# A four-layer block on one core: attention's output projection one unit later, skip terms and gate one slot later

## Chip, core and metric

One Trainium2 chip, one of its cores. The metric is the device time of one execution in microseconds (us), the median of the timed runs. A profile is one more execution, taken by the hardware profiler.

## What is computed

The program is a chain of four layers on an image batch x of shape 2 x 128 x 64 x 64 (channels first, 4096 pixels per image), all in float32. The change touches the first layer, a selective state-space network, and the second, attention. The third is attention with 1x1 projections, the fourth mixes four scales. Cut to what matters:

```
# layer 0, twice (two inner layers), t2 = layernorm(t)
u, z = split(t2 @ in_w.T);  u = silu(causal_conv4(u))
dt, Bm, Cm = split(u @ xproj_w.T);  dt = softplus(dt @ dt_w.T + dt_b)
h[t] = exp(dt[t]*A) * h[t-1] + dt[t]*u[t]*Bm[t]        # 256 channels x 16 states
y = sum_over_states(h * Cm) + u * ssm_D                # + skip term
t = t + (y * silu(z)) @ out_w.T                        # gate, mixer's output
t = t + gelu(layernorm(t) @ w1.T + b1) @ w2.T + b2
# layer 1
q, k, v = conv3x3(x)
attn = softmax(q.T @ k / sqrt(128));  out = attn @ v.T
x = x + Wo @ out + bo                                  # output projection
```

## The kernel before

**First layer (lines 111 to 533).** The pixels are cut into chunks of 512. An item is one image, one inner layer and one chunk: 32 items. The state runs on in the variable `carry` from chunk to chunk. An item has 32 slots, `t_` from 0 to 31. Every slot issues one scan (`scan`, VectorE, L384: 128 partitions are 32 channels times 4 states, 512 steps), and one exponential on ScalarE for the scan four slots ahead (`decay`, L373). Four slots make a group, 8 groups an item. At a group's end VectorE multiplies the next group's inputs (`times_b`, L366), into a tile `h` of which there are 5 buffers, and GpSimd saves the last column (L386) and multiplies the scanned states by C (L387). TensorE sums states two groups at a time (`y_pair`, L399, 8 matmuls, which are 16 instructions in the trace), which frees both groups' `h`, and spreads dt*u for a group into the one PSUM buffer `pdu` (`spread_dtu`, L360), which `times_b` of the group before has to have read.

All the rest of an item is *background*, given out by hand: `background(i)` fills a list for each of the 32 slots, and the loop at L514 issues, in every slot, first the scan's own work and then that list. All engines take their instructions in this order. In the lists, `n = i+1` is the item whose convolution is being prepared, `p = i-1` the one whose scan has just ended and `q = i-2` the one in the feed-forward part. The pieces that matter here:

- `y_out(i, j)` (L407, VectorE): skip term, `u = u*D + py`, for half j of the 256 channels. It needs all four groups of that half to have been summed by `y_pair`. Half 0 stands in the item's own slot 23, half 1 in slot 6 of the following item.
- `gate(p)` (L410, GpSimd): `z = z*u`, right behind half 1's `y_out`.
- `mix_out(p)` (L416 and L417, TensorE, slot 8): the mixer's output projection of the gated z, plus the residual by an identity matmul.
- `mix_add(p)` (L420, ScalarE, slot 10): copies it back into the image `xt`. Slot 11 holds `silu`, with two loads of activation tables.

**Attention (lines 547 to 863).** Four runs, two layers times two images, of 128 units; a unit is a quarter of the scores of 128 queries. Eight units make a group of 256 queries. Unit by unit the loop at L811 issues `score` (L709 on TensorE; VectorE copies PSUM out and takes maxima, L714), then the pieces of earlier groups: `product` (attention times v, L759), which lags 14 units, `exponentials`, `turn` (a transpose L739, then copies by GpSimd and DMAs from two queues), `divide` (L784, VectorE) in the unit with w = 5, where w is the unit's place in its group, and, in the first of the two layers only, `finish_mm` (L791, TensorE: Wo times the divided result `on`) and `finish` (L795, VectorE: bias and residual). In a unit, `finish_mm` comes behind the unit's scores and ahead of its `product`. Scores go through a pool of two PSUM buffers. Every 32 units, in the first layer, the inputs of the next 3x3 convolution are formed on VectorE in six consecutive units (L589 to L600).

**Last layer (lines 866 to 1233)** is not touched.

The order is the source's: `manual_schedule` keeps the instructions of every engine as written, and semaphores are put in where one engine needs another's result or a buffer.

Of the kernel before, what the change touches and what calls it, by code (L numbers as in the profile page):

```python
# [67 lines left out]
def tile_conv_seq(ctx: ExitStack, tc, x, consts, vecs, wemb, wlay, wconv, wdt, wqkv, wsmall, wms, out):  # L68
# [33 lines left out]
    def v1(name, i=0):  # L102
        return vec[:, VEC[name] + i : VEC[name] + i + 1]
# [7 lines left out]
    with ExitStack() as s, tc.manual_schedule():  # L111
# [25 lines left out]
        for l in range(NL):  # L137
            w = wp.tile([P, NWL - DI], F32, name=f"wl{l}")
# [7 lines left out]
            u = wp.tile([P, KC, DI], F32, name=f"wu{l}")  # L146
# [6 lines left out]
            for g in range(4):  # L153
                pa = mm.tile([P, NJ, DS], F32, name="pa", tag="mm")
                nc.tensor.matmul(pa.rearrange("p j n -> p (j n)"), lhsT=four(g), rhs=an, start=True, stop=True)
                for q in range(4):
                    at = slice(32 * q, 32 * q + 32)
# [38 lines left out]
        def has(i):  # L196
            return 0 <= i < NI
# [265 lines left out]
        def background(i):  # L463

            todo = [[] for _ in range(NSL)]

            def at(t, f, *a):
                todo[t].append((f, a))

            n, p, q, r = i + 1, i - 1, i - 2, i + 2  # L470
            if has(q):
                at(3, gelu, q)
                at(6, ffn_down, q, (0, 1)), at(7, ffn_down, q, (2, 3)), at(9, ffn_add, q)
                at(11, out_mm, q), at(12, out_add, q)
            if has(p):
                at(6, y_out, p, 1), at(6, gate, p)
                at(8, mix_out, p), at(10, mix_add, p)
            if has(n):
                at(0, pu_taps, n, 0, (0, 1)), at(1, pu_taps, n, 0, (2, 3)), at(2, pu_out, n, 0)
                at(3, pu_taps, n, 1, (0, 1)), at(4, pu_taps, n, 1, (2, 3)), at(5, pu_out, n, 1)  # L480
                at(13, xproj, n), at(14, xproj_out, n), at(14, spread_bc, n)
                at(15, dtproj, n, 0), at(16, dtproj, n, 1), at(17, soft_plus, n), at(18, dt_end, n)
            if has(i):
                at(1, pz_mm, i, 0), at(3, pz_out, i, 0)
                at(5, pz_mm, i, 1), at(6, pz_out, i, 1)
            if has(i) or has(n):
                at(11, silu, i, n)
            if i == -1:
                for k in range(3):
                    at(8 * k + 2, fold, k)  # L490
            pair = [(k, second) for k, second in ((p, True), (r, False)) if has(k)]
            if has(r):
                at(10, embed, r), at(11, embed_out, r)
            w, m = {}, len(pair)
            for k, (it, second) in enumerate(pair):
                at(12 + 2 * k, ln_centre, w, k, it)
                at(13 + 2 * k, ln_square, w, k, it)
                at(27, ln_spread, w, k, m), at(28, ln_scale, w, k, it)
                at(29, ln_shift, w, k, it, second)
            if pair:  # L500
                at(17, ln_var, w, m), at(18, ln_eps, w, m), at(19, ln_rs, w, m), at(20, ln_newton, w, m), at(21, ln_step, w, m)
            if has(p):
                for f in range(4):
                    at(30 + f // 2, ffn_up, p, f)
            if has(i):
                at(23, y_out, i, 0)
            return todo

        eps = wp.tile([P, 1], F32, name="eps")
# [36 lines left out]
    LAG = 14  # L546
    with ExitStack() as s, tc.manual_schedule():
# [22 lines left out]
        def load(which, half):  # L570
            slot = st["ring"] = (st.get("ring", -1) + 1) % 3
            where[which, half] = slot
            nc.sync.dma_start(uw[:, slot], ufold[which][:, 9 * half : 9 * half + 9, :])
# [82 lines left out]
        def keys(r):  # L656
            k = st["k"] = sp.tile([P, N], F32, name="k", tag="k")
            chunks(r, 1, lambda cc: k[:, cc * 4 * QG : (cc + 1) * 4 * QG])
# [27 lines left out]
        def queries(r, cc):  # L686

            for i in range(4):
                st["q", r, 4 * cc + i] = sp.tile([P, QG], F32, name="q", tag="q", bufs=5)
            outputs(*products(0), [st["q", r, 4 * cc + i] for i in range(4)], bias(r, 0))  # L690

        def query(r, grp):
            ps = psq.tile([P, QG], F32, name="pqq", tag="q")
            dense(r, 0, grp * QG, QG, ps)
            q = st["q", r, grp] = sp.tile([P, QG], F32, name="q", tag="q", bufs=5)
            put(q, ps, bias(r, 0))
# [19 lines left out]
        def exponentials(r, blk):  # L716
            scale = 1.0 if runs[r][0] else float(C) ** -0.5
            nm = sp.tile([P, 1], F32, name="nm", tag="nm", bufs=2)
            nc.vector.tensor_reduce(nm, st["mx"], AX.X, ALU.max)
            nc.vector.tensor_scalar(nm, nm, -scale, None, ALU.mult)  # L720
            sm = st["sm", r, blk] = sp.tile([P, 2], F32, name="sm", tag="sm", bufs=2)
            for hh in range(2):
                sc = st["sc", r, blk, hh]
                nc.scalar.activation(sc, sc, AF.Exp, bias=nm, scale=scale, accum_out=sm[:, hh : hh + 1])  # L724
# [49 lines left out]
        def xg(r, grp):  # L774
            l, b = runs[r]
            if l:
                k = QG // W
                return xt[:, b, 1 + grp * k : 1 + (grp + 1) * k, 1 : W + 1]
            cc, i = divmod(grp, 4)
            return xt[:, b, 1 + 16 * cc : 17 + 16 * cc, 1 + i : W + 1 : 4]  # L780
# [7 lines left out]
        def finish_mm(r, grp):  # L788
            if not runs[r][0]:
                st["p2", r, grp] = psm.tile([P, QG], F32, name="p2", tag="m")  # L790
                nc.tensor.matmul(st["p2", r, grp], lhsT=wa[:, WS_O : WS_O + C], rhs=st["on", r, grp], start=True, stop=True)  # L791

        def finish(r, grp):
            if not runs[r][0]:
                nc.vector.scalar_tensor_tensor(xg(r, grp), st.pop(("p2", r, grp)).rearrange("p (h w) -> p h w", w=16), v1("bo1"), xg(r, grp), ALU.add, ALU.add)  # L795

        def at(f, u0):

            r, u = divmod(now - u0, NU)
            if 0 <= r < len(runs):  # L800
                f(r, u)
# [9 lines left out]
        for now in range(NALL + LAG + 10):  # L811
            r, u = divmod(now, NU)
            w = now % 8
            if now < NALL:
                if u == 0:
                    if r == 2:
                        wm = wbig.tile([P, NS, 9, C], F32, name="wm", tag="wbig")
                        nc.sync.dma_start(wm, wms)
                    keys(r)
                    if runs[r][0]:  # L820
                        query(r, 0)

                r4, cc = divmod((now + 16) // 32, NCC)
                v = (now + 16) % 32
                if now >= 16 and r4 < B:
                    if v == 0:
                        ahead = inputs(r4, cc)
                    if v < 6:
                        for f in ahead[2 * v : 2 * v + 2]:
                            f()  # L830
                    if v == 14:
                        queries(r4, cc)
                        if r4 and cc == 0:
                            load(1, HI)
                score(r, u)
                if runs[r][0]:
                    if w == 2 and u // 8 + 1 < NU // 8:
                        query(r, u // 8 + 1)
                elif u == 1:
                    load(2, LO), load(2, HI)  # L840
                elif u == LAG:
                    load(0, LO), load(0, HI)
                    if r == 0:
                        load(1, LO)
            if w == 6:
                at(lambda r, u: finish_mm(r, u // 8), LAG + 8)
            at(product, LAG)
            if w == 6:
                at(lambda r, u: finish(r, u // 8), LAG + 8)
            if w in (3, 7):  # L850
                at(lambda r, u: exponentials(r, u // 4), 3)
            if w in (1, 5):
                at(lambda r, u: turn(r, u // 4, 0), 5)
            if w in (3, 7):
                at(lambda r, u: turn(r, u // 4, 1), 7)
            if w == 2:
                at(lambda r, u: diagonals(r, u // 8), 10)
            if w == 3:
                at(lambda r, u: spread(r, u // 8), 11)
            if w == 5:  # L860
                at(lambda r, u: divide(r, u // 8), LAG + 7)
            if now < NALL and u == LAG - 1:
                values(r)


    with ExitStack() as s, tc.manual_schedule():
# [51 lines left out]
        for si in (2, 3):  # L918
            wgt[si] = sp.tile([P, SCALES[si]], F32, name=f"wgt{si}")
            for k in range(SCALES[si]):  # L920
                w = (k + 0.5) / SCALES[si] - 0.5
# [393 lines left out]
```

## Time and profile before

| what | value |
|---|---|
| median of 3 runs | 5233.05 us (5232.73 to 5240.35) |
| profiled execution | span 5237.5 us, mean granted TensorE clock 0.931 |
| TensorE (PE) busy | 4755.4 us, 91% |
| VectorE (DVE) busy | 4094.0 us, 78% |
| ScalarE (ACT) busy | 2366.3 us, 45% |
| GpSimd (POOL) busy | 2310.8 us, 44% |
| `scan` L384 | 1024 of 1266 ns on average |
| `times_b` L366 | 256 of 2266 ns |
| states times C, L387 | 256 of 4532 ns |
| first layer's `y_out` | from 127.2 to 2144.9 us |
| first attention layer's L791 | from 2354.5 to 3472.3 us |

The first layer fills about the first 2160 us of the span, the two attention layers the stretch to about 4400, the last layer the rest. Busy shares are means over these stages. In a row of the timeline the columns are: start in us, length in us, engine, line, operation, what is written and read, sizes, how many instructions are merged in the row, and in brackets the engine's idle time before it with what ended it.

### The profile page before, as it was taken

Reading aid. Unit: us, or ns where it says so; the run is one execution under the profiler, and the core shown is the slowest. Engines: PE = TensorE matmul, PEld = TensorE weight load, DVE = VectorE, ACT = ScalarE, POOL = GpSimd, SP = SyncE. Lnnn points to the kernel's source line nnn. Section 1 sums busy time; section 2 is a strip of 40 time slices with the busy share of each in tenths; the row PEclk is TensorE's granted clock in tenths of the full one; section 3 lists DMA queues with packets and bytes.
Section 4 is the critical chain, followed back from the end, with each engine's and each line's share of the span. In section 5 each row is a group of like instructions: output and inputs, shape, how many; then the busy total and the mean of one; then the engine's idle time right before and its main releaser. Section 6 shows DMA issues by size and latency. Waiting matters only on the chain.

```text
span 5237.5 us, 48971 instructions
## 1 busy us (share of the span) xinstructions
PE 4755.4 (91%) x14797; PEld 2266.9 (43%) x14797; DVE 4094.0 (78%) x4416; ACT 2366.3 (45%) x3221; POOL 2310.8 (44%) x1948
## 2 busy tenths in 40 slices
PE   5899899999998998789999899999999998988997
PEld 1222222222222222356666666566666665332332
DVE  5999999999999899587777877667766775657665
ACT  4677777777777777322222222233333331322332
POOL 2766676666667667213332233323333333222321
PEclk8888988888889888899999999999999999999998
DMA  5322223333222323024443244434444442000000
GB/s 151 71 66 66 66 68 70 70 71 69 66 66 68 70 70 70 32 69 97 97 95 84 67 95 97 120 90 110 113 99 98 112 111 59 5 4 7 7 4 8
DMA packets 237015, 373.85 MB, mean 71 GB/s; under 512 B 88000, under 2 KB 88400, under 8 KB 228432
## 3 DMA queue, kind: packets, MB, share of 16 engines
q1 hardware_dynamic: 187600, 303.55, 24.4%
q10 hardware_dynamic: 49152, 67.17, 5.4%
q8 instruction: 118, 1.93, 0.2%
q14 instruction: 145, 1.19, 0.1%
HBM read 92.18 MB, written 9.83 MB: 19 GB/s over the span
## 4 chain that ended last, share of the span: by engine, by line
PE 51%; DVE 16%; POOL 14%; issue 8%; DMA 4%; SPq 3%; ACT 3%; DVEq 0%; ACTq 0%; POOLq 0%
PE po L759 11%; PE pq L709 11%; POOL h L387 11%; PE py L399 5%; DVE tr L739 5%; DMA pt<-tr 3%; PE pu L288 3%; SPq L750 3%; PE pf L1005 2%; PE pdu L360 2%; PE ph L429 2%; PE pqkv L1032 2%; DVE h L384 2%; PE pw L1087 1%; DVE h L366 1%
## 5 line engine op out<-in xcount | busy, mean ns | idle before, releaser
L746 POOL COPY pt<-tr 32x512 f32<-32x512 f32 x1024 | 651.8, 637 | 1560.5 <-DVE tr L739 771.8
L384 DVE TENSOR_TENSOR_SCAN h<-da,carry,h 128x512 f32<-128x512 f32 x1024 | 1241.3, 1266 | 51.9 <-ACT da L373 22.0
L387 POOL TENSOR_TENSOR h<-h,cb 128x2048 f32<-128x2048 f32 x256 | 1160.1, 4532 | 20.8 <-POOL carry L386 0.2
L759 PE MATMUL po<-pt,vt 128*128 128x256 f32 x4096 | 975.6, 382 | 2.4 <-DMA pt<-tr 2.4
L709 PE MATMUL pq<-k,q 128*128 128x512 f32 x2048 | 965.3, 594 | 8.5 <-DVE sc L714 6.2
L724 ACT ACTIVATE sc<-sc,nm 128x2048 f32<-128x2048 f32 x256 | 510.5, 1995 | 986.9 <-DVE nm L720 684.2
L714 DVE TENSOR_SCALAR_CACHE_REDUCE sc<-pq 128x1024 f32<-128x1024 f32 x512 | 625.5, 1222 | 419.3 <-PE pq L709 397.3
L759 PEld LDWEIGHTS po<-pt,vt 128*128 128x128 f32 x4096 | 783.5, 192 | 299.8 <-issue 212.3
L373 ACT ACTIVATE da<-dtb,am 128x512 f32<-128x512 f32 x1024 | 687.2, 685 | 274.8 <-DVE h L384 265.1
L739 DVE STREAM_TRANSPOSE tr<-sc 128x2048 f32<-128x2048 f32 x256 | 591.7, 2311 | 65.5 <-DMA pt<-tr 57.1
L366 DVE TENSOR_TENSOR h<-bb,pdu 128x2048 f32<-128x2048 f32 x256 | 580.0, 2266 | 39.9 <-issue 27.6
L399 PE MATMUL py<-h,sel 128*32 128x512 f32 x2048 | 521.4, 654 | 1.6 <-POOL h L387 1.6
L709 PEld LDWEIGHTS pq<-k,q 128*128 128x128 f32 x2048 | 384.7, 191 | 287.5 <-issue 248.5
L360 PE MATMUL pdu<-dtu,fsel 128*128 128x512 f32 x512 | 334.0, 739 | 124.8 <-DVE h L366 124.7
L399 PEld LDWEIGHTS py<-h,sel 128*32 128x32 f32 x2048 | 117.5, 120 | 429.0 <-issue 422.2
L288 PE MATMUL pu<-xn,wu 128*128 128x512 f32 x512 | 245.6, 613 | 3.5 <-ACT xn L278 1.9
L360 PEld LDWEIGHTS pdu<-dtu,fsel 128*128 128x128 f32 x512 | 96.9, 218 | 342.6 <-DVE h L366 219.6
L1032 PE MATMUL pqkv<-f,ws 128*128 128x512 f32 x384 | 198.8, 643 | 10.4 <-ACT q L1039 6.3
L1094 DVE TENSOR_TENSOR ov<-v,pw 128x2048 f32<-128x2048 f32 x64 | 146.2, 2284 | 63.5 <-PE pw L1087 63.4
L386 POOL COPY carry<-h 128x4 f32<-128x4 f32 x256 | 47.7, 186 | 317.8 <-DVE h L384 317.8
L1098 POOL TENSOR_TENSOR ov<-ov 128x2048 f32<-128x2048 f32 x16 | 72.6, 4540 | 257.2 <-DVE ov L1094 257.2
L1016 POOL TENSOR_SCALAR f<-lo 128x256 f32<-128x256 f32 x32 | 27.7, 865 | 323.7 <-PE po L1107 268.9
(241 smaller groups left out, 5429.8 us busy)
## 6 DMA issues: line engine op xcount, KB each, us to landing
pt<-tr SPq DMA_DIRECT2D x2048, 64.0 KB, 2.0
dtb<-dt SPq DMA_DIRECT2D x1024, 64.0 KB, 2.0
pt<-tr ACTq DMA_DIRECT2D x1024, 64.0 KB, 2.2
bb<-dr SPq DMA_DIRECT2D x128, 256.0 KB, 4.5
cb<-dr SPq DMA_DIRECT2D x128, 256.0 KB, 7.5
uw<-ufold SPq DMA_DIRECT2D x14, 576.0 KB, 3.9
xt<-in_x SPq DMA_DIRECT2D x16, 256.0 KB, 4.9
xr<-in_x SPq DMA_DIRECT2D x16, 256.0 KB, 2.9
```

Source lines behind the costliest of these rows:

```text
L360: nc.tensor.matmul(pdu, lhsT=four(s_ % 4), rhs=st[i]["dtu"][:, s_ // 4, :], start=True, stop=True)
L366: nc.vector.tensor_tensor(h, st[i]["bc", 0], pdu.unsqueeze(1).to_broadcast([P, 4, CH]), ALU.mult)
L373: nc.scalar.activation(da, st[i]["dtb", s_], AF.Exp, scale=am[items[i][1]][:, j, gg, m : m + 1])
L384: nc.vector.tensor_tensor_scan(h[:, m, :], da, h[:, m, :], carries[b, l][:, j, gg, m : m + 1], ALU.mult, ALU.add)
L387: nc.gpsimd.tensor_tensor(h, h, st[i]["bc", 1], ALU.mult)
L399: nc.tensor.matmul(py[r : r + 32, :], lhsT=sel, rhs=st[i]["h", s_ + k][:, m, :], start=(m == 0), stop=(m == 3), tile_position=(0, r),)
L709: nc.tensor.matmul(pq[:, i, :], lhsT=st["q", r, grp][:, it * P : (it + 1) * P], rhs=st["k"][:, at : at + CH], start=True, stop=True)
L714: nc.vector.tensor_scalar(dst, pq, 1.0, None, ALU.mult, ALU.max, accum_out=st["mx"][:, c2 : c2 + 1])
L724: nc.scalar.activation(sc, sc, AF.Exp, bias=nm, scale=scale, accum_out=sm[:, hh : hh + 1])
L739: nc.vector.transpose(tr, st.pop(("sc", r, blk, hh)).rearrange("p (t r f) -> p r t f", r=NB, f=32))
L746: nc.gpsimd.tensor_copy(dst, src)
L759: nc.tensor.matmul(st["po", r, grp], lhsT=st["vt"][:, jt, :], rhs=rhs, start=(jt == 0), stop=(jt == N // P - 1))
```

## The change

Two sets of places in the order are moved; no instruction is added or removed, and no size, buffer or data changes.

```diff
@@ background(i)
             if has(p):
-                at(6, y_out, p, 1), at(6, gate, p)
-                at(8, mix_out, p), at(10, mix_add, p)
+                at(7, y_out, p, 1), at(7, gate, p)
+                at(9, mix_out, p), at(11, mix_add, p)
@@
             if has(i):
-                at(23, y_out, i, 0)
+                at(24, y_out, i, 0)
@@ attention's loop over units
-            if w == 6:
-                at(lambda r, u: finish_mm(r, u // 8), LAG + 8)
+            if w == 7:
+                at(lambda r, u: finish_mm(r, u // 8), LAG + 9)
             at(product, LAG)
-            if w == 6:
-                at(lambda r, u: finish(r, u // 8), LAG + 8)
+            if w == 7:
+                at(lambda r, u: finish(r, u // 8), LAG + 9)
```

In the built program this comes to the following. On VectorE half 1's `y_out` passes one scan and one `times_b`, and half 0's passes one scan. On GpSimd the gate passes one L386 and one L387. On ScalarE `mix_add` passes one `decay`. On TensorE the first layer's order stays as it was, since slots 8 and 9 hold nothing else for it between the two places. In attention, L791 passes one unit's `product` (L759) and the next unit's scores (L709) on TensorE, and L795 passes one L714 on VectorE. The SyncE queue's order stays the same; no DMA of any queue is issued by a moved piece.

## The prediction

> **What bounds it now.** I read the waits by engine first, because the change only moves work within queues:
>
> ```profile
> DVE sc L714 <- PE pq L709: 397.3, 238, 15.6
> DVE u L407 <- PE py L399: 92.1, 58, 8.6
> PE pdu L360 <- DVE h L366: 124.7, 55, 5.1
> PE p L791 <- DVE on L784: 45.2, 23, 3.9
> POOL z L410 <- DVE u L407: 125.3, 32, 4.6
> ```
>
> Columns: total us, times, longest. Two waits are the change's targets: VectorE before `y_out` (92.1 us, 1.6 each on average) and TensorE before `finish_mm` (45.2 us). Neither total is a gain yet; whether it is depends on who waits next. So I read one first-layer item (851 to 916; scan starts 64.85 apart) engine by engine:
>
> ```profile
> 863.83 0.75 DVE L407 SCALAR_TENSOR_TENSOR u<-u,vec,py 128x512 f32<-128x512 f32 x1 [2.16 <-PE py L399]
> 864.50 1.28 DVE L384 TENSOR_TENSOR_SCAN h<-da,carry,h 128x512 f32<-128x512 f32 x1
> 865.69 2.26 DVE L366 TENSOR_TENSOR h<-bb,pdu 128x2048 f32<-128x2048 f32 x1
> ...
> 893.97 1.28 DVE L384 TENSOR_TENSOR_SCAN h<-da,carry,h 128x512 f32<-128x512 f32 x1 [1.01 <-ACT da L373]
> 895.17 2.26 DVE L366 TENSOR_TENSOR h<-bb,pdu 128x2048 f32<-128x2048 f32 x1
> 898.25 0.75 DVE L407 SCALAR_TENSOR_TENSOR u<-u,vec,py 128x512 f32<-128x512 f32 x1 [0.81 <-PE py L399]
> ```
>
> ```profile
> 860.13 3.63 PE L399 MATMUL py<-h,sel 128*32 128x512 f32 x16
> ...
> 871.71 1.88 PE L416 MATMUL po<-z,wl 128*128 128x512 f32 x4
> ...
> 889.08 3.58 PE L236 MATMUL var<-sq,kc 128*2 128x512 f32 x4 [1.28 <-ACT dt L341]
> ...
> 905.95 2.07 PE L360 MATMUL pdu<-dtu,fsel 128*128 128x512 f32 x2 [3.09 <-DVE h L366]
> ```
>
> ```profile
> 874.48 0.59 ACT L420 COPY xt<-po 128x512 f32<-128x512 f32 x1 [2.05 <-PE po L417]
> 874.97 0.70 ACT L373 ACTIVATE da<-dtb,am 128x512 f32<-128x512 f32 x1
> ```
>
> ```profile
> 856.10 4.55 POOL L387 TENSOR_TENSOR h<-h,cb 128x2048 f32<-128x2048 f32 x1
> 864.66 2.37 POOL L410 TENSOR_TENSOR z<-z,u 128x1024 f32<-128x1024 f32 x1 [4.02 <-DVE u L407]
> ```
>
> To be seen: TensorE has no wait from 905.95 through the next item's start to the wait before L236. So the item's period is a loop: TensorE from `pdu` (slot 28) to the mixer's output, ScalarE without a pause from `mix_add` to the softplus that L236 waits for, TensorE to `py`, VectorE from half 0's `y_out` over four scans and one `times_b` to `pdu` again. Half 1's 2.16 us is not in this loop: VectorE is held again later, by `da` (1.01).
>
> In attention one finish reads:
>
> ```profile
> 2742.37 1.98 PE L709 MATMUL pq<-k,q 128*128 128x512 f32 x4 [0.23 <-DVE sc L714]
> 2748.25 1.19 PE L791 MATMUL p<-on,wa 128*128 128x256 f32 x2 [3.89 <-DVE on L784]
> 2749.23 2.92 PE L759 MATMUL po<-pt,vt 128*128 128x256 f32 x8
> ```
>
> TensorE stands idle for a result VectorE gives at 2748.1, while L759 behind it, which does not need it, could run.
>
> **What the Trainium skill says.** "PSUM — Partial Sum Buffer", section "Engine vs sequencer instructions": ScalarE, VectorE and GpSimd queues are strict FIFO and matmuls keep program order. The trace agrees: L759 starts only behind L791. "TensorE: Matmul & The Clock Gate", section "What's actually happening": TensorE runs at half clock after an idle window of about 3.4 us and at full clock after a busy one. The trace agrees: the granted clock is 0.50 from 887.6 to 894.45 and from 901.27 to 911.5, 1.00 between and after, all steps multiples of 3.41 us; and L759 took 2.92 us behind the long wait, 1.89 otherwise. "GPSIMD Engine Reference", section "3.1 Elementwise — side-by-side cycle accounting", gives 4497 ns for a product of two tensors of 2048 float32; L387 took 4532 here. It prices what the gate now stands behind.
>
> **Part by part, first layer.**
>
> Half 1's `y_out` (slot 6 to 7). The scan of slot 7 (1.2 us) now runs inside the wait. The next `times_b`, though, needs an `h` buffer, and counting five buffers back (8 groups and one feed-forward tile an item) it is the one that the same `py` (ending 863.76) frees. So about 0.95 of the 2.16 us stays, ahead of L366 now; VectorE is 1.2 us earlier for slots 8 to 15. Given back: `pdu` and `da` hold it at slots 19 to 23. Worth 0 on the loop; bounds 0 and 1.2.
>
> Gate behind one L386 and L387. The slot 7 scan ends near 862.9, L387 runs 863.2 to 867.7, the gate to 870.1. `mix_out` starts at 871.71: 1.6 us to spare, cost 0. Its upper bound is in the slow rival. L387 itself comes earlier; `times_b` is not waiting for it there.
>
> `mix_out` keeps its place on TensorE: 0. `mix_add` behind one `decay`: ScalarE now idles 2.05 us ahead of it, and that decay's buffer (slot 11's scan, ending about 871.7 then) is free in time, so 0.6 us moves from behind the copy into the wait. Items in which TensorE then is no later than ScalarE get 0.6; with the layer's last matmuls (L455, L456) present, as in this item, ScalarE's copy of `pd` waits for TensorE anyway and 0.1 is left.
>
> Half 0's `y_out` (slot 23 to 24): the scan of slot 24 fills its 0.81 us, so 0.5 to 0.8. GpSimd's chain from softplus over L347, L387 and L252 to the `da` of slot 25 allows no more.
>
> Sum on the loop: 16 items at 1.2, 8 like this one at 0.6, 4 with both embedding and last matmuls at 0.2 (there GpSimd's chain already held `da`): 19.2 + 4.8 + 0.8 = 25 us. The other four, at the ends, have slack: 0.
>
> Clock. After `pdu` restarts at 905.95 the half clock holds until 911.5, 5.56 us, which loses 2.8. Restarting anywhere in a window loses between 1.3 and 3.0, 2.3 on average by the windows seen. The item's period has settled on 19 windows (19 x 3.413 = 64.85). A shorter loop leaves that phase; I take 0.3 us for 28 items, 8 us, bounds -0.5 and +1.5 each. First layer: 33 us. The clock's bounds make it 11 to 67; with what half 1 might give or the loop might not, 0 and 75.
>
> **Attention.** 32 finishes, 23 with a wait: 16 of about 1.1 us and 7 of 3.9. One unit later TensorE first does a `product` and a `score`, 1.72 us each back to back, 3.44. The 16 short waits vanish: 17.9 us. They are exposed now: groups take 29.8 us, and eight units of 3.44 plus L770 and L791 are 28.6. The seven long waits keep about 0.4: 24.5 us. They lie where VectorE is full (convolution inputs). The work moved forward needs no VectorE result: scores have their buffer since 2744.9, and the scores after them theirs at 2749.2. Each long wait is also followed by half clock, 5 times 3.41 and twice 6.83 us, 30.7 in all, losing 15.4; half of that, 8, since part of the idling stays. L795 (0.68 us) now stands ahead of the negated maximum (L719, L720) and a transpose with its copies and DMAs; it passes one L714 (1.22), which gains. ScalarE's exponentials start 0.7 us later, and the next reader of them is two units away: 0. `on` and the PSUM buffer shared with L770 are needed four or more units later: 0. Sum: 50 us, bounds 20 (VectorE takes the long ones back) and 60.
>
> Together 83 us of the profiled 5237.5. That execution was timed at 5239.27, the runs at 5232.73 to 5240.35, median 5233.05; 5233 - 83 = 5150.
>
> **Rivals.**
>
> *The clock's windows hold the item.* Periods come back to 64.85 from both sides (64.37, 64.89, 64.86, 64.85 in four items running). If the restart only shifts within its window, half clock eats the 1.2: first layer 0, time 5233 - 50 = 5183. Against it: the loop without half clock would lie too low for the largest loss (3.0) to refill it.
>
> *VectorE takes attention's long waits back*, being busy all through 2724 to 2749: attention 20, time 5233 - 33 - 20 = 5180.
>
> *All waits are gained*: 92 + 45 + 15 of half clock = 152, time 5081. Against it: half 1's wait is off the loop.
>
> *Slower: the gate comes late.* If L387 of slot 7 starts only when `y_out` ends (866.85), the gate ends 4.72 + 2.37 later at 873.9, and TensorE waits 2.2 us at `mix_out`; with a half-clock window after it (1.7) that is 3.9, in 30 items 117 us. Less 50 in attention and with nothing gained elsewhere: 5300. It decides from 871.7 on, 1.6 us later than I place the gate's end. Against it: GpSimd is idle 4.02 us just there.
>
> *Nothing measurable*: both waits are replaced by equal ones (`h` buffers; the next scores): 5233, give or take 10.
>
> **Chances.** Likeliest case 0.58 (first layer 20 to 65, attention 38 to 53, so 5115 to 5175), clock 0.14, VectorE 0.10, all gained 0.08: faster 0.90. Nothing 0.05, slower 0.05. A measurement here tells about 0.2%, 10.5 us, from no change. The range, 5100 to 5200, takes in the clock and VectorE rivals and leaves out the last two and most of the full gain.
>
> **What would show it.** Right: L407's waits for `py` near 0, about 1 us a time ahead of L366 in slot 7, no wait of L416 for the gate, L791 waiting under 5 us in all, no half-clock windows behind finishes, attention groups near 28.7 us, items between 62 and 64. Wrong: items still at 64.85, L416 waiting for L410, or new waits of L709 for L714 in attention as large as those removed.

## The result, and the profile after

| kernel | median | runs | ratio to before, 95% interval |
|---|---|---|---|
| before | 5235.95 us | 4, 5232.73 to 5240.35 | |
| after | 5142.68 us | 4, 5142.37 to 5143.39 | 0.9822 [0.9804, 0.9839] |

The change makes the kernel 93 us faster; the forecast was 83. The runs of the kernel before spread over 10 us (5230.7 to 5241.0 in the largest set), so differences of a few us are read from the traces here and not from medians alone. The profiled execution went from a span of 5237.5 to 5141.6 us and from a granted clock of 0.931 to 0.941. Cut at the last scan, at attention's first score and at the first score of the second attention layer, the 95.9 us of the two spans lie here:

| stage | before | after | difference |
|---|---|---|---|
| to the end of the scans | 2136.3 | 2101.7 | -34.6 |
| to attention's first score | 100.5 | 100.8 | +0.3 |
| first attention layer | 1165.4 | 1107.9 | -57.5 |
| second attention layer, to its last score | 956.2 | 952.8 | -3.4 |
| rest | 879.0 | 878.5 | -0.5 |

The waits of the kernel after (engine, line and what it waited for: total us, times, longest):

```profile
DVE sc L714 <- PE pq L709: 339.9, 231, 14.2
PE pdu L360 <- DVE h L366: 101.6, 53, 5.1
DVE h L366 <- PE py L399: 29.3, 27, 2.7
DVE u L407 <- PE py L399: 8.6, 1, 8.6
POOL z L410 <- DVE u L407: 5.4, 2, 4.5
PE po L416 <- POOL z L410: 3.8, 1, 3.8
PE p L791 <- DVE on L784: 3.2, 7, 0.5
```

`y_out`'s 58 waits have become one, at the very end of the layer. Of what stood ahead of it, 29.3 us stands ahead of `times_b` now: 27 times 1.08 us. L791's 45.2 us have become seven waits of 0.46. VectorE's wait for scores has become shorter too (397.3 to 339.9), and TensorE's wait for L714 ahead of its scores is 6.2 us in both kernels, so VectorE took nothing back. The same first-layer item as before, on VectorE, TensorE, GpSimd and ScalarE:

```profile
849.95 2.29 DVE L366 TENSOR_TENSOR h<-bb,pdu 128x2048 f32<-128x2048 f32 x1 [1.36 <-PE py L399]
852.15 0.74 DVE L407 SCALAR_TENSOR_TENSOR u<-u,vec,py 128x512 f32<-128x512 f32 x1
...
883.13 1.28 DVE L384 TENSOR_TENSOR_SCAN h<-da,carry,h 128x512 f32<-128x512 f32 x1
884.33 0.72 DVE L407 SCALAR_TENSOR_TENSOR u<-u,vec,py 128x512 f32<-128x512 f32 x1
```

```profile
857.44 1.88 PE L416 MATMUL po<-z,wl 128*128 128x512 f32 x4
...
890.83 2.08 PE L360 MATMUL pdu<-dtu,fsel 128*128 128x512 f32 x2 [2.94 <-DVE h L366]
```

```profile
848.92 4.55 POOL L387 TENSOR_TENSOR h<-h,cb 128x2048 f32<-128x2048 f32 x1
853.41 2.37 POOL L410 TENSOR_TENSOR z<-z,u 128x1024 f32<-128x1024 f32 x1
```

```profile
860.22 0.59 ACT L420 COPY xt<-po 128x512 f32<-128x512 f32 x1 [1.55 <-PE po L417]
```

Both `y_out` start without a wait. The gate starts behind L387 at once and ends at 855.78; `mix_out` starts at 857.44, 1.66 us later, where the forecast had 1.6. ScalarE still idles ahead of `mix_add`, 1.55 us instead of 2.05. A finish in attention that had one of the long waits now reads:

```profile
2687.05 1.88 PE L709 MATMUL pq<-k,q 128*128 128x512 f32 x4
2689.38 0.67 PE L791 MATMUL p<-on,wa 128*128 128x256 f32 x2 [0.45 <-DVE on L784]
2689.89 1.89 PE L759 MATMUL po<-pt,vt 128*128 128x256 f32 x8
```

L759 behind it takes 1.89 us again, not 2.92: no half clock follows any of the seven finishes. In the chain of waits that ended last, L387's share of the whole span has risen from 11% to 17% and GpSimd's from 14% to 21%:

```profile
PE 45%; POOL 21%; DVE 13%; issue 11%; ACT 4%; DMA 3%; SPq 2%; ACTq 0%; DVEq 0%; POOLq 0%
POOL h L387 17%; PE po L759 13%; PE pq L709 13%; DVE tr L739 3%; PE pf L1005 2%; DMA pt<-tr 2%; SPq L750 2%; PE pqkv L1032 2%; PE py L399 2%; PE pw L1087 1%; POOL z L410 1%; POOL dtu L347 1%; PE psc L1052 1%; DVE h L384 1%; PE pfus L1152 1%
```

Between 84 and 2100 us L387 makes up 42.3% of the chain, in the kernel before 26.2%. In the item above it runs over L347, L387, L252, L257 and L387 again; the forecast had named L347, L387 and L252, up to the `da` of slot 25, as the next limit. That GpSimd holds the items now is not shown beyond this: another 24.8% of the stretch is "issue", time whose cause the profile doesn't show, and no run shortens GpSimd's work.

### The profile page after: what moved, and what is told of

It reads as the page before. It is cut to its first block, busy times and chain, and to the rows that moved or that the text cites. A ratio compares the mean times of both kernels' runs of the same rounds, so it can differ in the third digit from the quotient of the medians.

```text
span 5141.6 us, 48961 instructions
## 1 busy us (share of the span) xinstructions
PE 4702.8 (91%) x14797; PEld 2255.8 (44%) x14797; DVE 4093.2 (80%) x4416; ACT 2367.5 (46%) x3221; POOL 2313.1 (45%) x1948
## 3 DMA queue, kind: packets, MB, share of 16 engines
q14 instruction: 145, 1.19, 0.1%
## 4 chain that ended last, share of the span: by engine, by line
PE 45%; POOL 21%; DVE 13%; issue 11%; ACT 4%; DMA 3%; SPq 2%; ACTq 0%; DVEq 0%; POOLq 0%
POOL h L387 17%; PE po L759 13%; PE pq L709 13%; DVE tr L739 3%; PE pf L1005 2%; DMA pt<-tr 2%; SPq L750 2%; PE pqkv L1032 2%; PE py L399 2%; PE pw L1087 1%; POOL z L410 1%; POOL dtu L347 1%; PE psc L1052 1%; DVE h L384 1%; PE pfus L1152 1%
## 5 line engine op out<-in xcount | busy, mean ns | idle before, releaser
L384 DVE TENSOR_TENSOR_SCAN h<-da,carry,h 128x512 f32<-128x512 f32 x1024 | 1241.5, 1266 | 59.1 <-ACT da L373 30.2
L387 POOL TENSOR_TENSOR h<-h,cb 128x2048 f32<-128x2048 f32 x256 | 1161.0, 4535 | 20.9 <-POOL carry L386 0.2
L709 PE MATMUL pq<-k,q 128*128 128x512 f32 x2048 | 963.9, 594 | 8.6 <-DVE sc L714 6.2
L759 PE MATMUL po<-pt,vt 128*128 128x256 f32 x4096 | 967.3, 379 | 2.4 <-DMA pt<-tr 2.4
L714 DVE TENSOR_SCALAR_CACHE_REDUCE sc<-pq 128x1024 f32<-128x1024 f32 x512 | 624.9, 1222 | 361.5 <-PE pq L709 339.9
L759 PEld LDWEIGHTS po<-pt,vt 128*128 128x128 f32 x4096 | 779.1, 190 | 295.2 <-issue 211.3
L366 DVE TENSOR_TENSOR h<-bb,pdu 128x2048 f32<-128x2048 f32 x256 | 581.7, 2272 | 77.4 <-PE py L399 29.3
L399 PE MATMUL py<-h,sel 128*32 128x512 f32 x2048 | 510.8, 642 | 1.6 <-POOL h L387 1.6
L709 PEld LDWEIGHTS pq<-k,q 128*128 128x128 f32 x2048 | 383.6, 190 | 286.7 <-issue 247.7
L386 POOL COPY carry<-h 128x4 f32<-128x4 f32 x256 | 47.9, 187 | 387.7 <-DVE h L384 385.9
```

Source lines behind the costliest of these rows:

```text
L366: nc.vector.tensor_tensor(h, st[i]["bc", 0], pdu.unsqueeze(1).to_broadcast([P, 4, CH]), ALU.mult)
L384: nc.vector.tensor_tensor_scan(h[:, m, :], da, h[:, m, :], carries[b, l][:, j, gg, m : m + 1], ALU.mult, ALU.add)
L387: nc.gpsimd.tensor_tensor(h, h, st[i]["bc", 1], ALU.mult)
L399: nc.tensor.matmul(py[r : r + 32, :], lhsT=sel, rhs=st[i]["h", s_ + k][:, m, :], start=(m == 0), stop=(m == 3), tile_position=(0, r),)
L709: nc.tensor.matmul(pq[:, i, :], lhsT=st["q", r, grp][:, it * P : (it + 1) * P], rhs=st["k"][:, at : at + CH], start=True, stop=True)
L714: nc.vector.tensor_scalar(dst, pq, 1.0, None, ALU.mult, ALU.max, accum_out=st["mx"][:, c2 : c2 + 1])
```

## The experiments

**The first layer's three moves, one at a time.** Theory: half 0's `y_out` and `mix_add` are on the loop, half 1's `y_out` is not. Rival: gains follow the waits that go, so half 1's move, with the most wait, brings most.

All three without attention's:

```diff
-                at(6, y_out, p, 1), at(6, gate, p)
-                at(8, mix_out, p), at(10, mix_add, p)
+                at(7, y_out, p, 1), at(7, gate, p)
+                at(9, mix_out, p), at(11, mix_add, p)
...
-                at(23, y_out, i, 0)
+                at(24, y_out, i, 0)
```

> The first layer's four moves without attention's. Theory (two independent gains): 35 us less than before, within 4, and attention's stage as before. Rival (part of the 93 us comes from both moves together, or the clock's phase is carried over): under 28 or over 42 us less.

Measured: 5201.53 against 5237.37 us, ratio 0.9937 [0.9924, 0.9949]: 36 us. With the 62 us that attention's move gives alone (below) this makes 98, where both together gave 93; the spread of the kernel before covers the difference.

Half 0's `y_out` alone:

```diff
-                at(23, y_out, i, 0)
+                at(24, y_out, i, 0)
```

> Of the change, half 0's skip term alone (slot 23 to 24). Theory (it lies on the item's loop through TensorE, ScalarE and VectorE): about 0.6 us of an item's loop goes, which takes the items off 19 clock windows; 10 to 27 us less than before. Rival (what counts is the wait in front of the skip terms, 2.16 us for half 1 and 0.81 for half 0): its share of the 35 us by waits, 9 to 10 us.

Measured: 5213.74 us, 0.9960 [0.9947, 0.9974]: 24 us. Its row of L407, which was 92.1 in 58 places before:

```profile
DVE u L407 <- PE py L399: 72.8, 32, 8.6
```

That is 19.3 us less in 26 places. By the periods in the table below, the 24 items that gain became 23.0 us shorter in sum and the four at the ends 2.0 us longer, so the move gave about the wait it removed or a little more; the interval of the runs (14 to 28 us) doesn't tell which.

Half 1's `y_out` and the gate alone:

```diff
-                at(6, y_out, p, 1), at(6, gate, p)
+                at(7, y_out, p, 1), at(7, gate, p)
```

> Half 1's skip term and the gate alone (slot 6 to 7). Theory (VectorE is held again later in the item by ScalarE and TensorE, so this wait is off the loop): within 4 us of before, with the 2.16 us turned into about 1 us ahead of L366 and longer waits for pdu and da later. Rival (the waits that vanish are gains): 1.2 us in 28 items, 34 us less, nearly all of the first layer's gain.

Measured: 5235.27 us, 1.0001 [0.9992, 1.0009]: nothing. Its waits on VectorE, and behind them two of the kernel before:

```profile
DVE h L384 <- ACT da L373: 35.1, 58, 1.9
DVE h L366 <- PE py L399: 29.1, 27, 2.6
DVE u L407 <- PE py L399: 29.1, 27, 8.6
DVE h L366 <- PE pdu L360: 22.3, 50, 0.8
```

```profile
DVE h L384 <- ACT da L373: 22.0, 32, 1.1
DVE h L366 <- PE pdu L360: 4.8, 7, 1.3
```

L407's total fell by 63.0 us (from 92.1), and 59.7 came back: 29.1 ahead of `times_b` for `py`, where there was no such row before, 17.5 more for `pdu` (from 4.8) and 13.1 more for `da` (from 22.0). A wait off the loop was moved, not removed.

`mix_add` (with `mix_out`, which keeps its place on TensorE) alone:

```diff
-                at(8, mix_out, p), at(10, mix_add, p)
+                at(9, mix_out, p), at(11, mix_add, p)
```

> The mixer's output and its copy alone (slots 8 and 10 to 9 and 11), which only moves the copy L420 behind one more exponential on ScalarE. Theory (ScalarE between this copy and the softplus is on the loop): 0.6 us in 16 items, with the clock's windows 6 to 20 us less than before, although every wait of L407 stays. Rival (only the skip terms' waits matter): 0, within 3.

Measured: 5224.98 us, 0.9977 [0.9967, 0.9986]: 12 us. Nearly all of VectorE's wait for `py` stayed; ScalarE's wait ahead of the copy, 60.7 us in 30 places before, shrank by more than half:

```profile
DVE u L407 <- PE py L399: 87.8, 49, 8.6
ACT xt L420 <- PE po L417: 27.0, 30, 1.9
```

The three alone sum to 2 + 24 + 12 = 38 us, together 36, each known to 5 to 7 us. Mean period of an item, from scan start to scan start, by what stands in it beside the rest (us):

| | embedding only (8 items) | last matmuls only (8) | both (4) | neither (8) | ends (4) |
|---|---|---|---|---|---|
| before | 64.75 | 64.86 | 64.89 | 63.99 | 60.91 |
| half 1 alone | 64.71 | 64.87 | 64.89 | 63.99 | 60.75 |
| half 0 alone | 63.89 | 63.72 | 64.94 | 63.12 | 61.41 |
| `mix_add` alone | 63.56 | 64.90 | 64.91 | 63.40 | 60.96 |
| after | 63.15 | 63.72 | 64.86 | 62.44 | 60.80 |

`mix_add` gives nothing where the last matmuls stand, half 0 gives in all but the four items with both and the ends, and half 1 nowhere.

**Attention's move alone, and half of it.** First the attention part of the change without the first layer's (the diff's second part: w of 7 and `LAG + 9`).

> Attention's output projection one unit later, the first layer as before. Theory: 42 us of waits of L791 and 15 us of half clock behind the seven long ones go: 58 us less than before, within 4. Rival (the half clock comes from elsewhere and VectorE takes part of the waits back): 30 to 45 us less.

Measured: 5173.87 against 5236.13 us, 0.9883 [0.9866, 0.9899]: 62 us. Seven waits of 0.46 us are left, and no half clock behind them.

Then the kernel before with `finish_mm` only put behind the same unit's `product`:

```diff
-            if w == 6:
-                at(lambda r, u: finish_mm(r, u // 8), LAG + 8)
             at(product, LAG)
+            if w == 6:
+                at(lambda r, u: finish_mm(r, u // 8), LAG + 8)
```

> L791 in its old unit, but behind that unit's product L759 instead of ahead of it: half of the shift, 1.72 us. L795 keeps its place. Theory (the shift covers what is shorter than itself, and a half-clock window follows only when TensorE idles most of one): the 16 waits of 1.1 us vanish, the seven of 3.9 leave 2.2, so 18 + 12 = 30 us less, and 30 to 45 with what half clock goes. Rival (only a full unit's shift helps since the scores of the next unit have to be ahead): under 20 us less.

Measured: 5198.68 us, 0.9927 [0.9912, 0.9942]: 37.5 us. One finish of it:

```profile
2734.93 0.67 PE L791 MATMUL p<-on,wa 128*128 128x256 f32 x2 [2.17 <-DVE on L784]
2735.44 3.52 PE L709 MATMUL pq<-k,q 128*128 128x512 f32 x4
```

A `product` of 1.72 us cuts the wait of 3.90 to 2.17, seven times the same, and all short waits are gone. Behind each of the seven one 3.41 us stretch of half clock is left (L709 takes 3.52 us instead of 1.88). So even a wait of 2.2 us brought a whole step of half clock here, seven times of seven, and one of 0.46 none. The idle window of about 3.4 us from which the prediction started isn't needed for it, and the measurement decides. The length of a wait alone doesn't settle it either. TensorE waits 2.81 us at the same place, ahead of L669, in the kernel before and in the kernel after:

```profile
3460.50 1.28 PE L669 MATMUL pvt<-kc,vs 128*128 128x128 f32 x8 [2.81 <-ACT vs L561]
3367.21 1.09 PE L669 MATMUL pvt<-kc,vs 128*128 128x128 f32 x8 [2.81 <-ACT vs L561]
```

In the first trace the clock is 0.50 from 3461.27 to 3464.68, in the second it stays at 1.00. All changes of the clock in these two traces lie on a grid of 3.413 us; that it matters how a wait lies to this grid would explain the difference, but no run here tests it.

**An operation more behind half 0's `y_out`.** If that place is on the loop, work put there must be lost. To the kernel before, and to the kernel after:

```diff
             nc.vector.scalar_tensor_tensor(u, u, vl("ssm_D", i, j), st[i].pop(("py", j)), ALU.mult, ALU.add)
+            if j == 0:
+                nc.vector.scalar_tensor_tensor(u, u, 1.0, u, ALU.mult, ALU.max)
```

> The kernel before with one more VectorE instruction an item, behind half 0's skip term and in place on the same 128x512 (u = max(1.0*u, u), which changes no value): about 0.6 us on the item's loop, 32 times. Theory (the items are held at 19 clock windows, and half clock gives way by as much as is added, up to about 1 us): the 20 items at 64.85 stay there, the others lose, so 0 to 8 us more than before. Rival (the loop has no such give): 0.6 x 28 = 17 us more, within 3.

Measured: 5248.06 us, 1.0024 [1.0014, 1.0034]: 12 us more, between the two expectations. The 20 items with embedding or last matmuls lost nothing (their sum fell by 1.5); those with neither lost 8.3 us and the ends 7.3. The operation took 1.17 us on average, and not the 0.6 that I had counted.

> The changed kernel with the same added instruction. Theory (its loop is free of the 19 windows, so that the added time shows, and part of its items fall back to 64.85): 12 to 25 us more than the changed kernel, that is 68 to 81 us less than before. Rival (no windows): about the same loss as the same instruction brings in the kernel before, 17 us in both; rival (half 0's skip term is off the loop here): under 5 us.

Measured: 5179.80 us, 0.9892 [0.9878, 0.9907] to before, so 37 us more than the kernel after. I had expected 12 to 25. The operation was longer than I thought, 1.16 us on average, and the items with embedding fell back to 64.80 us. In the trace of the kernel after with it:

```profile
385.90 1.26 POOL L257 TENSOR_TENSOR rs<-rs,nt 2x512 f32<-2x512 f32 x1 [0.83 <-ACT nt L253]
386.56 1.15 DVE L409 SCALAR_TENSOR_TENSOR u<-u 128x512 f32<-128x512 f32 x1
387.11 0.64 POOL L386 COPY carry<-h 128x4 f32<-128x4 f32 x1
```

L257 ends at 387.16 and L409 at 387.71, 0.55 us later; L386 took 0.19 us elsewhere. So I ran one more, with the second input from PSUM (`py`) in place of SBUF (`u`):

```diff
+                nc.vector.scalar_tensor_tensor(u, u, 1.0, py, ALU.mult, ALU.max)
```

> The change with one VectorE operation added behind half 0's y_out, as in after_plus_op, but with py in PSUM as its second input in place of u in SBUF: u = max(u, py), which changes the layer's output. It should take about 0.7 us every time, where the SBUF operation took 1.15 in the middle and always ended 0.55 us after the GpSimd instruction that ran when it started. after_plus_op cost 37 us more than the changed kernel. Theory 1 (the lock-out made it cost that: the added op waited for GpSimd, and GpSimd's L386 and L387 behind it came later too): 10 to 22 us more than the changed kernel. Theory 2 (any delay of this size on the loop drops the items back to 19 clock windows): 30 to 40 us more, and embedding items at 64.7 to 64.9.

Measured: 5159.28 us, 0.9854 [0.9837, 0.9870] to before: 16.6 us more than the kernel after, embedding items at 63.52. Its row:

```profile
L410 DVE SCALAR_TENSOR_TENSOR u<-u,py 128x512 f32<-128x512 f32 x32 | 22.0, 687 | 1.1
```

That is 0.69 us in each of 32 items, and the loss is about what 24 of them carry (24 x 0.69 = 16.6), unevenly: 0.37 us an item with embedding, 0.95 with last matmuls, 0.74 with neither. The place is on the loop in the kernel after. Theory 2 fails for a delay of 0.69 us. Theory 1 fits, but it is not shown for all of the other 20 us: with SBUF the 32 operations took 37.1 us together instead of 22.0, and the half clock in an item with embedding rose from 11.52 us to 15.79, with PSUM only to 11.95. The waiting for GpSimd and the clock's part are not separated by these runs.

**Further in the same direction.** ScalarE's remaining 1.55 us ahead of `mix_add`:

```diff
-                at(9, mix_out, p), at(11, mix_add, p)
+                at(9, mix_out, p), at(11 if has(q) and items[q][1] == 1 and has(r) and items[r][1] == 0 else 12, mix_add, p)
```

> The change with mix_add one slot further back still, behind silu and its two table loads in slot 12; in the four items with both an embedding product and last matmuls it stays where it is. In the changed kernel ScalarE still idles about 1.5 us ahead of the copy L420. Theory (ScalarE's chain from mix_add to the softplus is part of the loop, so filling its idle time shortens the loop): 5 to 15 us less than the changed kernel, the gain in the items without last matmuls. Rival (GpSimd's chain from the softplus over L347, L387 and L252 to da now holds the items, or the clock's windows do): within 3 us of the changed kernel.

Measured: 5138.22 us (5134.38 to 5138.45), 0.9810 [0.9797, 0.9824] to before: 4.5 us less than after, between the theory (5 to 15) and the rival (within 3), and no more than the spread of its own runs. In the trace the gain lies where the theory had it: items with embedding went from 63.15 to 62.66, those with neither from 62.44 to 61.95, those with last matmuls stayed. The wait went and another took most of its place:

```profile
ACT sq L229 <- PE pc L222: 40.5, 35, 2.4
ACT xt L420 <- PE po L417: 6.2, 4, 1.6
```

The wait ahead of the copy was 50.3 us in the kernel after and that of L229 9.7. L222 needs the copied `xt`, so a later copy makes its reader late.

Attention's finish one unit later still:

```diff
-            if w == 7:
-                at(lambda r, u: finish_mm(r, u // 8), LAG + 9)
+            if w == 0:
+                at(lambda r, u: finish_mm(r, u // 8), LAG + 10)
...
-            if w == 7:
-                at(lambda r, u: finish(r, u // 8), LAG + 9)
+            if w == 0:
+                at(lambda r, u: finish(r, u // 8), LAG + 10)
```

> The change with attention's finish_mm and finish one more unit later (w of 0, two units behind the place they had before). Theory (only seven waits of about 0.46 us were left at L791, and no half clock behind them): those waits go, 3 us less than the changed kernel, 1 to 5. Rival (further delay takes buffers or VectorE's time that something else needs): 2 to 10 us more than the changed kernel.

Measured: 5137.60 us (5136.91 to 5138.05), 0.9810 [0.9797, 0.9823]: 5.1 us less than after. TensorE waits nowhere for L784. The seven groups of units in which a wait of 0.46 us stood became 0.8 to 1.1 us shorter each, so the wait as listed was only a part of what the finish cost (the section on the prediction says why).

> Both of the further moves together. Theory: the gains add, since they lie in different stages: 8 to 18 us less than the changed kernel. Rival: within 3 us of the changed kernel.

Measured: 5130.57 us (5128.83 to 5132.07), 0.9797 [0.9783, 0.9810] to before: 12.1 us less than the changed kernel (each measured against before in its own set of runs). This is the fastest version I have.

## Why the prediction was right, step by step

The mechanism was right in both stages; the 10 us between 83 and 93 lie in sizes, nearly all of them in attention.

**The loop, 25 us.** TensorE's restart at `pdu` (slot 28), measured from the item's start, is the end of the loop's first part; what follows it contains the half clock. Means by kind:

| | restart before | after | earlier by | forecast | rest of the item shorter by | half clock after the restart shorter by |
|---|---|---|---|---|---|---|
| embedding | 54.89 | 53.70 | 1.19 | 1.2 | 0.41 | 0.81 |
| last matmuls | 55.00 | 54.14 | 0.86 | 0.6 | 0.27 | 0.56 |
| both | 54.81 | 54.80 | 0.01 | 0.2 | 0.03 | 0.05 |
| neither | 53.86 | 52.87 | 0.99 | 1.2 | 0.55 | 0.82 |

8 x 1.19 + 8 x 0.86 + 8 x 0.99 = 24.3 us. Each kind is off by up to 0.3, the sum by less than 1, and in part that is luck: of the two terms of 0.6 in an item with embedding, `mix_add` alone brought the restart 0.90 earlier and half 0 alone 0.61, together only 1.19; with neither they brought 0.54 and 0.42. In the items with last matmuls half 0's move alone brought the restart to 54.28, 0.72 earlier, within its 0.5 to 0.8.

**The clock, 8 us.** 8 x 0.41 + 8 x 0.27 + 4 x 0.03 + 8 x 0.55 = 10 us, and in the first three kinds it is half of the half clock that went. The prediction's reason is seen too: between the restart and full clock 1.80 to 2.95 us were lost in the 28 items before, 2.68 on average, as the restart stood near one place in the step of the clock; after the change it is 1.49 to 3.14, 2.36 on average, where the prediction had 2.3 for a restart anywhere. The periods of the kernel after keep no single phase: embedding items alternate between about 63.7 and 62.6 (mean 63.15, or 18.5 steps of 3.413 us).

**Half 1's `y_out`, 0 on the loop.** Confirmed by its run alone, and 1.08 us a time (forecast 0.95) stands ahead of `times_b`.

**Attention, 50 us.** The first attention layer gave 57.5, and the first two groups of the second 2.8 more, 60.3 in all. Two terms of the sum were too small.

The short waits, 17.9 us. The 16 groups with such a wait became 22.1 us shorter, 29.8 to 28.4 each. The profile counts a wait from the end of the matmul before, but matmuls overlap: those of L709 take 0.59 us each and start 0.43 apart. In the kernel before:

```profile
2711.98 1.88 PE L709 MATMUL pq<-k,q 128*128 128x512 f32 x4
2714.96 0.67 PE L791 MATMUL p<-on,wa 128*128 128x256 f32 x2 [1.10 <-DVE on L784]
```

Back to back, the next matmul starts 1.72 us after the first of these four, at 2713.70. L791 started at 2714.96, 1.26 us later and not 1.10, and its two matmuls started 0.29 us apart instead of 0.22.

The half clock, 8 us, "since part of the idling stays". None of it stayed: behind 0.46 us of waiting the clock is full. The seven groups with a long wait became 37.2 us shorter; 24.1 of this is the wait (7 x 3.44), which leaves about 13 for the clock and the overlap. That is less than the 15.4 that the prediction had put at most, as two of the stretches began over 1 us before L791 did, while TensorE stood idle.

The last group gave 1.4 without any wait of L791: one more stretch of half clock, behind the wait of L669 shown above, is gone from it. Its wait is the same, so this gain is luck as far as the change is concerned; in the kernel with the finish two units later that group is 1.4 us longer again. Two other groups became 0.5 us longer together.

**Rivals.** The windows did not hold the item: with only the first layer's part, embedding items were at 63.13. Something like it is seen when the loop gets longer: with the added operation in the kernel before, half clock in an item with embedding fell from 16.64 to 13.65 us, in one with last matmuls from 17.07 to 13.65, and their periods stayed at 64.67 and 64.71 on average. Single items then went from 64.27 to 65.73, so they were not held one by one. The rival failed here, where the loop became shorter; about a small lengthening it would have been nearer. VectorE took back nothing in attention. All waits gained (5081) failed at half 1, as argued. The late gate happened once, in the second item of the layer: L416 waited 3.8 us.

## What to carry to other kernels

Follow a wait to the engine that waits next before you count it: 63 us of waits removed were worth nothing where the same buffers held the engine one instruction later, and 12 us came from a copy that hardly changed the largest wait. Where TensorE stands idle for a few us, look in the trace for half clock behind it and count that as part of the wait: here it stood behind every wait of 2.17 and 3.9 us at L791 and behind none of 0.46, but behind the 2.81 us at L669 only in one of two kernels. Count what a wait costs TensorE from the start of one matmul to the start of the next: listed waits of 1.10 us were worth 1.4. A finish whose operands come from another engine cost TensorE no wait here once two units of other work stood ahead of it.

## What the runs showed that I had not expected

**VectorE was locked out by GpSimd.** The added operation with both inputs in SBUF took 0.69 us alone, but wherever an L252, L257 or L387 was running when it started, it ended 0.55 us after that instruction: 1.15 us in the middle, 3.49 at most; GpSimd's L386, issued during it, took 0.64 us instead of 0.19. With one input in PSUM it took 0.69 every time. The Trainium skill, "SBUF — State Buffer", section "SBUF: two separate sides", says that a VectorE operation with two SBUF inputs and a GpSimd operation that reads SBUF exclude each other for a whole instruction, and that the one that starts first goes ahead. This agrees. The scans L384 agree as well: they read `h` from SBUF but `da` from PSUM, and in the kernel after they took 1.26 us (median of 729) where they began under a GpSimd instruction of over 1 us and 1.26 (of 265) where none ran, never over 1.29.

**The same operation cost 12 us in the kernel before and 37 after.** In the kernel before, the 20 items that took 64.7 to 64.9 us on average took it in without a loss in sum, and those of them with embedding or last matmuls alone had 3.0 and 3.4 us less of half clock each. At half speed that is 1.5 and 1.7 us of TensorE's time, against the 1.15 and 1.13 us that the operation took in them. In the kernel after, the items were shorter than that and became longer, with embedding from 63.15 to 64.80. That the clock gave the time back in the first case, and took some in the second, fits these sums; it is not shown by a run of its own.
